# The last layer of a four-layer graph kernel: bursts of five units in place of three, placed by a table of bursts

## Chip, cores and metric

The kernel runs on one core of a Trainium2 chip. The metric is the device time of one launch in microseconds (us), as the median of the runs. Smaller is better.

## What is computed

The input is x, 16 batches of 1024 nodes with 64 features in float32, and one 1024 x 1024 adjacency matrix that all batches share. Four graph layers follow one another, each added to its input and layer-normalized. The change touches the fourth alone, layer 3. For each batch it computes (the reference, cut):

```python
def _gat_layer(h, mask, b):
    scores = jnp.einsum('...nd,...md->...nm', h, h)
    scores = jnp.where(mask, scores, NEG)
    attn = jax.nn.softmax(scores, axis=-1)
    return jnp.einsum('...nm,...md->...nd', attn, h) + b
mask = graph + jnp.eye(N, dtype=graph.dtype) > 0
h = jnp.einsum('bnc,hdc->bhnd', x, Wh)                  # 4 heads of 64
out_h = _gat_layer(h, mask[None, None], bh[None, :, None, :])
cat = jnp.transpose(out_h, (0, 2, 1, 3)).reshape(B, N, H * D)
z = jax.nn.leaky_relu(cat, negative_slope=0.2)
h2 = jnp.einsum('bnk,dk->bnd', z, Wo)
out2 = _gat_layer(h2, mask[None], bo)                   # the outer attention
z2 = jax.nn.leaky_relu(out2, negative_slope=0.2)
# layernorm of z2 with gamma and beta; then x = layernorm(x + that)
```

## The kernel before

The function that matters is `fast_path`. Layers 0 to 2 take the first 684 us. Layer 3 works on units. A unit is a tile of 128 x 1024 attention weights. It passes through three engines, and in the code each pass has its own step:

- `scores` (L1281 for heads, L1378 for the outer attention): TensorE (PE) makes the scores of the unit as two products with 64 rows each, which lie in the two halves of its array and run side by side. They go to a two-bank PSUM tile `s`, of which there are three. ScalarE (ACT) then takes the exponential into a tile `e` (L1285, L1383), with a shift that was worked out beforehand.
- the mask: VectorE (DVE) multiplies `e` with the adjacency `aT` (L1286; L1385 for outer units, there into a second tile `me`). For outer units a second DVE instruction, `add_up` (L1396), adds up the unmasked tile against the adjacency `aN` to get the softmax's denominators.
- `product` (L1293, L1405): PE multiplies the masked tile with the values, as two products with 64 columns each, and adds them up over 8 units in a PSUM tile `y`.

A batch has 32 head units (2 pairs of heads, 2 halves of the queries, 8 tiles of keys) and 8 outer units. The outer units of a batch stand among the head units of the next batch, since they need all of its heads. `tile e` has 9 buffers in a ring, used for `e`, for `me`, and in batch 0 for the adjacency tiles that `nodes_adj` loads again.

Between the units stand small tasks. `prep_x`, `prep_h` and `prep_sq` make the head features of a pair of batches; `shift_of` makes the shift (PE L1218, DVE L1222, a maximum over partitions on GpSimd L1224, and one small DVE instruction L1229); `project` (L1310 to L1320, then `leaky`) divides and leaves z; `z_T`, `h_2T`, `h_2v` (L1339, L1351, L1364) prepare the outer attention; `gather`, `layer`, `mean`, `centre`, `scale`, `affine`, `residual`, `finish` end a batch on DVE. `scale` asks ACT for a logarithm and an exponential (L702, L703). Most of them that use PE take one of the three `s` tiles.

The order on every engine of PE, ACT, DVE and GpSimd is the order in which the code issues, written out by hand. `run` takes units in bursts of three:

```python
catch_up()
made = [(unit[1], unit[0]()) for _, _, unit in burst if unit]   # scores, exp, mask
for b, p, _ in burst:
    tasks(mids, b, p)
drain()                          # the products of the burst before
```

So PE does three scores, then tasks listed as `mids`, then the three products of the burst before, then tasks listed as `slots`. `catch_up` runs, ahead of the next scores, what was left in the list `soon`: the last step of a shift, and the root and Newton step of a `scale`. The positions of tasks are counted in units, 40 to a batch. The outer unit comes after every second head unit from position 18 on (in the last batch after every one).

Of the kernel before, what the change touches and what calls it, by code (L numbers as in the profile page):

```python
# [8 lines left out]
F32 = mybir.dt.float32  # L9
F32R = mybir.dt.float32r  # L10
BF16 = mybir.dt.bfloat16
# [5 lines left out]
P = 128  # L17
# [561 lines left out]
def fast_path(  # L579
# [87 lines left out]

    soon = []
    in_order = {getattr(mybir.EngineType, e) for e in ("PE", "Activation", "DVE", "Pool")}
# [43 lines left out]
    def normalizing(y, sq, late):  # L713
# [15 lines left out]
        def scale():  # L729
            vs = small.tile([P, n], F32, tag="ln_vs", name="ln_vs")  # L730
            nc.vector.tensor_reduce(vs, sq, AX.X, ALU.add)
            ve = small.tile([P, n], F32, tag="ln_ve", name="ln_ve")
            nc.vector.tensor_scalar(ve, vs, 1.0 / D, LN_EPS, ALU.mult, ALU.add)
            rstd = small.tile([P, n], F32, tag="ln_rstd", name="ln_rstd")
            if late:
                nc.gpsimd.tensor_tensor(rstd, ve, neg_half, ALU.pow)
                return rstd
            root, step = inverse_root(rstd, ve)

            def first():  # L740
                root()
                soon.append(step)

            soon.append(first)
            return rstd
# [452 lines left out]
    def nodes_adj(c):  # L1198
        a_sb = l3.tile([P, N], I32, tag="e", name=f"adj3_{c}", bufs=9)
        nc.sync.dma_start(a_sb, adj_v[c])  # L1200
# [12 lines left out]
    def shift_of(key, sq):  # L1213
# [14 lines left out]
        def below():  # L1228
            nc.vector.tensor_scalar(sh, gtop, -1.0, HEADROOM, ALU.mult, ALU.add)  # L1229

# [41 lines left out]
    def heads(b, n):  # L1272
        held = {}

        def scores(k, h):
# [3 lines left out]
            for i in range(2):  # L1279
# [3 lines left out]
                )  # L1283
            e = l3.tile([P, 2, HALF], F32, tag="e", name="e", bufs=9)
            nc.scalar.activation(e, s, AF.Exp, bias=shifts[b, n])  # L1285
            nc.vector.tensor_tensor(e, e, bc_mid(aT[:, k, cols], 2), ALU.mult)  # L1286
            return e

        def product(k, h, e):
# [7 lines left out]
            if k == C - 1:  # L1297
                if h == 0:
                    held["y"] = l3.tile([P, N], F32, tag="y", name=f"yT_{b}_{n}")
                nc.scalar.copy(held["y"][:, h * HALF : (h + 1) * HALF], held[h])  # L1300

        def project(q):
# [5 lines left out]
            for j in range(CH):  # L1308
                c = q * CH + j
                nc.tensor.matmul(  # L1310
                    o[:, j // 2, j % 2, :], held["y"][:, c * P : (c + 1) * P], wb[:, n, :], start=True, stop=True,
                )
# [5 lines left out]
            for i in range(2):  # L1318
# [6 lines left out]

        units = [(lambda k=k, h=h: scores(k, h), lambda e, k=k, h=h: product(k, h, e), None)
                 for h in range(2) for k in range(C)]
        return units, project


    def prep_out(b):
# [28 lines left out]
        def h_2v():  # L1360
            v = l3.tile([P, C, D], F32, tag="h2v", name=f"h2v_{b}", bufs=1)
            pt = one_bank("ph2v").rearrange("p (c d) -> p c d", c=C)
            for c in range(C):
                nc.tensor.transpose(pt[:, c, :], hTs[b][0][:D, c // CH, c % CH * P : (c % CH + 1) * P], ident[:D, :D])  # L1364
            nc.vector.tensor_copy(v, pt)  # L1365
            vals["out", b] = v
# [3 lines left out]
    def head_out(b):  # L1370
        held = {}

        def scores(k):
            s = ps_s.tile([P, 2, HALF], F32, tag="s", name="s")
            hT = hTs[b][0]
            for i in range(2):
# [4 lines left out]
                )  # L1381
            e = l3.tile([P, 2, HALF], F32, tag="e", name="e", bufs=9)
            nc.scalar.activation(e, s, AF.Exp, bias=shifts[b])  # L1383
            m = l3.tile([P, 2, HALF], F32, tag="e", name="me", bufs=9)
            nc.vector.tensor_tensor(  # L1385
                m, e, aT[:, k, :].rearrange("p (i q) -> p i q", i=2), ALU.mult
            )
            return e, m

        def unit(k):  # L1390
            held[k], m = scores(k)
            return m

        def add_up(k):
            junk = l3.tile([P, N], BF16, tag="junk", name="junk", bufs=1)
            nc.vector.scalar_tensor_tensor(  # L1396
                junk, held.pop(k).rearrange("p i q -> p (i q)"), 1.0, aN[:, k, :], ALU.mult, ALU.mult,
                accum_out=sums[:, b, H, k : k + 1],
            )

# [55 lines left out]
        def finish():  # L1456
# [4 lines left out]
        units = [  # L1461
            (lambda k=k: unit(k), lambda e, k=k: product(k, e), lambda k=k: add_up(k)) for k in range(C)
        ]
# [150 lines left out]


    slots, mids = {}, {}
    work = [[heads(b, n) for n in range(NP)] for b in range(B)]
    outs = [(prep_out(b), head_out(b)) for b in range(B)]
    BURST = 3
    LAST = 40  # L1620
    E = B - 1

    def at(b, p, task, where=slots):
        where.setdefault((b, p), []).append(task)

    for c in range(C):
        convert = {}
        at(0, 2 * c, lambda c=c, convert=convert: convert.update(go=nodes_adj(c)))
        at(0, 2 * c + 5, lambda convert=convert: convert["go"]())
    for b in range(B):  # L1630
# [6 lines left out]
        ends = outs[b][1][1]  # L1637
        if b < E:
            places = [13, 22, 26, 33, LAST + 4, LAST + 7, LAST + 10, LAST + 13, LAST + 14]

            end = (41, 46, 49, 55) if b < E - 2 else (29, 31, 33, 39)
            places += [2 * LAST + p for p in (6, 8, 10, 11, 14, 23, 25, *end)]
        else:
            places = [13, 22, 26, 35, *[LAST - 1] * 5, *[LAST + 8] * 11]
        if b == E - 1:
            places[9:] = [LAST + 38, *[LAST + 39] * 4, *[2 * LAST + p for p in (3, 3, 3, 3, 3, 8)]]
        for task, p in zip(chain + ends, places):
            t = min(p // LAST, max(E - b, 0))
            at(b + t, p - t * LAST, task)


    ended = slots[E, LAST - 1]
    slots[E, LAST - 1] = [ended[i] for i in (5, 0, 1, 6, 2, 3, 7, 8, 9, 4)]
    ahead = []
    for b in range(0, B, 2):
        for t, p, task, where in (
            (-1, 16, lambda b=b: prep_x(b), slots),
            (-1, 20, lambda b=b: prep_h(b, 0, 0), mids), (-1, 23, lambda b=b: prep_sq(b, 0, 0), slots),
            (-1, 26, lambda b=b: prep_h(b, 0, 1), mids), (-1, 29, lambda b=b: prep_sq(b, 0, 1), slots),
            (-1, 25, lambda b=b: prep_v(b), slots),  # L1660
            (-1, 32, lambda b=b: shift_of((b, 0), hTs[b, 0][1]), slots),
            (-1, 36, lambda b=b: shift_of((b + 1, 0), hTs[b + 1, 0][1]), slots),
            (0, 2, lambda b=b: prep_h(b, 1, 0), mids), (0, 3, lambda b=b: prep_sq(b, 1, 0), slots),
            (0, 5, lambda b=b: prep_h(b, 1, 1), mids), (0, 8, lambda b=b: prep_sq(b, 1, 1), slots),
            (0, 11, lambda b=b: shift_of((b, 1), hTs[b, 1][1]), slots),
            (0, 20, lambda b=b: shift_of((b + 1, 1), hTs[b + 1, 1][1]), slots),
            (0, 19, lambda b=b: prep_v(b + 1), slots),
        ):
            if b + t < 0:
                ahead.append(task)  # L1670
            else:
                at(b + t, p, task, where)

    with tc.tile_pool(name="ps_g", bufs=1, space=bass.MemoryType.PSUM, reuse_waits="tile") as ps_g, tc.tile_pool(
# [13 lines left out]
        ending = gat_layer(later["w2"], "l2", True, extra, first, 5, True)  # L1688
    for p, task in zip((1, 4, 7, 10, 14, 16), ending):
        at(0, p, task)  # L1690

# [16 lines left out]

    queue = []
    for b in range(B):  # L1710
        units = work[b][0][0] + work[b][1][0]
        outer = outs[b - 1][1][0] if b else [None] * C
        for i, unit in enumerate(outer):
            units.insert(18 + (3 if b < E else 2) * i, unit)
        queue += [(b, p, unit) for p, unit in enumerate(units)]
    last = [(E, LAST + p, unit) for p, unit in enumerate(outs[E][1][0])]

    def run(queue):
        while queue:
            burst = []  # L1720
            while queue and sum(unit is not None for _, _, unit in burst) < BURST:
                burst.append(queue.pop(0))
            catch_up()
            made = [(unit[1], unit[0]()) for _, _, unit in burst if unit]
            for b, p, _ in burst:
                tasks(mids, b, p)
            drain()
            waiting.extend(lambda product=product, e=e: product(e) for product, e in made)
            if not queue:
                drain()  # L1730
            for b, p, _ in burst:
                tasks(slots, b, p)
            for _, _, unit in burst:
                if unit and unit[2]:
                    unit[2]()

    with tc.manual_schedule(engines=in_order):
        run(queue)
        run(last)
        for task in [catch_up, *slots[E, LAST + 8]]:  # L1740
            task()
            while soon:
                catch_up()

# [72 lines left out]
```

## Time and profile before

| | us |
|---|---|
| median of 3 runs | 2126.72 (2126.08 to 2129.75) |
| the profiled execution, its own time | 2126.6 |
| its span | 2124.7 |
| PE busy in the span | 1998.2 (94%) |
| DVE busy | 1858.1 (87%) |
| ACT busy | 1228.0 (58%) |
| stretch 684 to 1974, batches 0 to 14 of layer 3: PE busy of 1290 | 1267.7 |
| same stretch, DVE busy / ACT busy | 1113.9 / 791.9 |
| stretch 1974 to 2066, last batch: PE / DVE busy of 92 | 89.3 / 84.6 |
| stretch 2066 to the end: PE / DVE busy of 58.7 | 23.2 / 46.8 |

A row of the page such as "L1285 ACT ACTIVATE e<-s,shift ... x512 | 542.8, 1111 | 242.8 <-PE s L1281 237.4" reads: line 1285 of the kernel, on ACT, writes e from s and shift, 512 times; 542.8 us busy, 1111 ns each; ACT was idle for 242.8 us before these, mostly until PE had finished an s. PE is matmuls, PEld is TensorE's weight loads, which overlap them. PEld idle "<-issue" is time in which nothing that the profile shows was waited for. DMA hardly matters in layer 3 (1 to 12 GB/s).

### The profile page before, as it was taken

What the parts mean: (1) busy time and instruction counts of PE and PEld (TensorE: products, weight loads), DVE (VectorE), ACT (ScalarE), POOL (GpSimd) and SP (SyncE); (2) the same over time, 40 slices, a digit from 0 to 9 for tenths busy, and PEclk for the clock granted to TensorE, in tenths of its full rate; (3) what the DMA queues carried; (4) which work ended last, traced back from release to release, by engine and by line L of the source; (5) the groups of instructions that cost most, each with busy time, mean ns of one, the idle gap of its engine ahead of it and who ended that gap; (6) DMA issues with size and microseconds to landing.
All of it is one profiled execution on the core that took longest, in us unless ns stands there. A gap on an engine that the chain in (4) does not pass through costs nothing.

```text
span 2124.7 us, 26159 instructions
## 1 busy us (share of the span) xinstructions
PE 1998.2 (94%) x10065; PEld 845.2 (40%) x10065; DVE 1858.1 (87%) x3224; ACT 1228.0 (58%) x1965; POOL 55.6 (3%) x77
## 2 busy tenths in 40 slices
PE   7999979988898999999999999999999999999993
PEld 3444447753332333333333333333333333333331
DVE  5888989989999867898888898889889889889997
ACT  4355566555556756556656655655665666565541
POOL 0000000000000000000000000000000000000001
PEclk7999989999989999999999999999999999999997
DMA  6000000000000100000000000000000000000000
GB/s 165 1 1 1 1 1 1 1 0 1 1 1 31 50 1 1 1 1 6 6 1 6 1 6 6 1 6 1 6 6 1 6 1 6 6 1 6 6 6 12
DMA packets 23654, 18.89 MB, mean 9 GB/s; under 512 B 19361, under 2 KB 19426, under 8 KB 23522
## 3 DMA queue, kind: packets, MB, share of 16 engines
q1 hardware_dynamic: 23218, 17.11, 2.7%
q8 instruction: 81, 1.33, 0.3%
q14 instruction: 51, 0.42, 0.1%
q10 hardware_dynamic: 304, 0.03, 0.0%
HBM read 12.95 MB, written 4.19 MB: 8 GB/s over the span
## 4 chain that ended last, share of the span: by engine, by line
PE 68%; DVE 26%; ACT 4%; issue 1%; DMA 0%; POOL 0%; SPq 0%; POOLq 0%; DVEq 0%; ACTq 0%
PE y L1293 19%; PE s L1281 17%; DVE e L964 7%; PE y_l L976 6%; PE s L1378 5%; PE y L1405 4%; DVE e L1286 4%; PE po L1310 3%; PE u_l L988 3%; PE po L1567 3%; ACT e L1285 1%; DVE r L1576 1%; PE pzT L1339 1%; PE phT L1255 1%; DVE junk L1396 1%
## 5 line engine op out<-in xcount | busy, mean ns | idle before, releaser
L1285 ACT ACTIVATE e<-s,shift 128x1024 f32<-128x1024 f32 x512 | 542.8, 1111 | 242.8 <-PE s L1281 237.4
L1286 DVE TENSOR_TENSOR e<-e,aT 128x1024 f32<-128x1024 f32 x512 | 602.5, 1220 | 87.2 <-ACT e L1285 85.1
L1281 PE MATMUL s<-hT 64*128 64x512 f32 x2048 | 508.9, 610 | 16.0 <-DVE top L1222 8.8
L1293 PE MATMUL y<-e,vals 128*64 128x512 f32 x2048 | 490.6, 601 | 3.2 <-ACT yT L1300 1.3
L964 DVE SCALAR_TENSOR_TENSOR e<-G_l,q,aT 128x1024 f32<-128x1024 f32 x256 | 315.4, 1278 | 7.2 <-ACT G_l L945 7.2
L976 PE MATMUL y_l<-e,vals_l 128*64 128x512 f32 x1024 | 263.6, 639 | 23.8 <-DVE e L964 23.0
L1281 PEld LDWEIGHTS s<-hT 64*128 64x128 f32 x2048 | 181.8, 186 | 256.3 <-issue 169.2
L1293 PEld LDWEIGHTS y<-e,vals 128*64 128x64 f32 x2048 | 131.0, 136 | 330.6 <-issue 257.7
L1383 ACT ACTIVATE e<-s,shift 128x1024 f32<-128x1024 f32 x128 | 141.7, 1112 | 84.8 <-PE s L1378 74.9
L1385 DVE TENSOR_TENSOR me<-e,aT 128x1024 f32<-128x1024 f32 x128 | 155.8, 1220 | 16.8 <-ACT e L1383 16.5
L1396 DVE SCALAR_TENSOR_TENSOR junk<-e,aN 128x1024 bf16<-128x1024 f32 x128 | 156.0, 1219 | 0.2
L1405 PE MATMUL y<-me,h2v 128*64 128x512 f32 x512 | 135.3, 609 | 10.6 <-DVE me L1385 10.4
L1378 PE MATMUL s<-h2T 64*128 64x512 f32 x512 | 136.3, 610 | 4.6 <-DVE h2v L1365 4.4
L976 PEld LDWEIGHTS y_l<-e,vals_l 128*64 128x64 f32 x1024 | 65.6, 142 | 162.2 <-issue 75.0
L1567 PE MATMUL po<-hi,aR 128*128 128x512 f32 x256 | 101.9, 398 | 2.7 <-ACT hi L1552 1.1
L1567 PE MATMUL po<-lo,aR 128*128 128x512 f32 x256 | 99.8, 390 | 0.0
L775 ACT ACTIVATE x<-m,bn_shift,bn_rstd 128x64 f32<-128x64 f32 x256 | 88.2, 429 | 0.0
L1340 ACT COPY zT<-pzT 128x1024 f32<-128x1024 f32 x32 | 32.4, 1013 | 78.4 <-PE pzT L1339 78.4
L1310 PEld LDWEIGHTS po<-wb,yT 128*128 128x128 f32 x512 | 62.0, 190 | 34.0 <-issue 21.1
L1310 PE MATMUL po<-wb,yT 128*128 128x130 f32 x512 | 73.8, 287 | 1.3 <-ACT e L1285 1.2
L1378 PEld LDWEIGHTS s<-h2T 64*128 64x128 f32 x512 | 46.6, 186 | 63.7 <-issue 41.4
L1405 PEld LDWEIGHTS y<-me,h2v 128*64 128x64 f32 x512 | 32.7, 137 | 93.8 <-issue 56.1
(214 smaller groups left out, 2003.7 us busy)
## 6 DMA issues: line engine op xcount, KB each, us to landing
adj<-in_adj_dram SPq DMA_DIRECT2D x16, 512.0 KB, 4.5
x<-in_x_dram SPq DMA_DIRECT2D x16, 256.0 KB, 5.0
out_dram<-res SPq DMA_DIRECT2D x16, 256.0 KB, 2.0
wl<-in_L_gnn_Wh_dram SPq DMA_DIRECT2D x2, 64.0 KB, 4.8
wo<-in_L_gnn_Wo_dram SPq DMA_DIRECT2D x1, 64.0 KB, 4.4
l_wd<-in_L_gnn_W_dram ACTq DMA_DIRECT2D x2, 16.0 KB, 4.7
l_wd<-in_L_gnn_W_dram SPq DMA_DIRECT2D x2, 16.0 KB, 2.1
bo<-in_L_gnn_bo_dram SPq DMA_DIRECT2D x1, 32.0 KB, 3.1
```

The source lines that it names most:

```text
L964: nc.vector.scalar_tensor_tensor(e, G[b - b % 2][:, b % 2, :], pq[b - b % 2][1][:, k, b % 2 : b % 2 + 1], aT[:, k, :], ALU.max, ALU.mult,)
L976: nc.tensor.matmul(held["y"][h * D : (h + 1) * D, :], vals[b][:, k, :], e[:, h * HALF : (h + 1) * HALF], start=(k == 0), stop=(k == C - 1),)
L1281: nc.tensor.matmul(s[:, i, :], hT[rows, k * P : (k + 1) * P], hT[rows, cols], start=True, stop=True)
L1285: nc.scalar.activation(e, s, AF.Exp, bias=shifts[b, n])
L1286: nc.vector.tensor_tensor(e, e, bc_mid(aT[:, k, cols], 2), ALU.mult)
L1293: nc.tensor.matmul(held[h][i * D : (i + 1) * D, :], vals[b][:, k, :], e[:, i, :], start=(k == 0), stop=(k == C - 1),)
L1310: nc.tensor.matmul(o[:, j // 2, j % 2, :], held["y"][:, c * P : (c + 1) * P], wb[:, n, :], start=True, stop=True,)
L1378: nc.tensor.matmul(s[:, i, :], hT[rows, (i + k // CH) % 2, k % CH * P : (k % CH + 1) * P], hT[rows, 0, :], start=True, stop=True,)
L1385: nc.vector.tensor_tensor(m, e, aT[:, k, :].rearrange("p (i q) -> p i q", i=2), ALU.mult)
L1396: nc.vector.scalar_tensor_tensor(junk, held.pop(k).rearrange("p i q -> p (i q)"), 1.0, aN[:, k, :], ALU.mult, ALU.mult, accum_out=sums[:, ...
L1405: nc.tensor.matmul(held["o"][h * D : (h + 1) * D, :], vals["out", b][:, k, :], e[:, h, :], start=(k == 0), stop=(k == C - 1),)
L1567: nc.tensor.matmul(po.rearrange("p q k f -> p (q k f)"), aR[:, k, ic * P : (ic + 1) * P], e[:, k].rearrange("p q k f -> p (q k f)"), start ...
```

## The change

Layer 3 is staged anew. Its core (lines with "..." are left out):

```diff
-            nc.vector.tensor_scalar(sh, gtop, -1.0, HEADROOM, ALU.mult, ALU.add)
+            nc.scalar.activation(sh, gtop, AF.Identity, bias=headroom, scale=-1.0)
...
-            e = l3.tile([P, 2, HALF], F32, tag="e", name="e", bufs=9)
+            e = l3.tile([P, 2, HALF], F32, tag="e", name="e", bufs=11)
             nc.scalar.activation(e, s, AF.Exp, bias=shifts[b, n])
-            nc.vector.tensor_tensor(e, e, bc_mid(aT[:, k, cols], 2), ALU.mult)
+            return e
+
+        def mask(k, h, e):
+            nc.vector.tensor_tensor(e, e, bc_mid(aT[:, k, h * HALF : (h + 1) * HALF], 2), ALU.mult)
             return e
...
-                if h == 0:
-                    held["y"] = l3.tile([P, N], F32, tag="y", name=f"yT_{b}_{n}")
-                nc.scalar.copy(held["y"][:, h * HALF : (h + 1) * HALF], held[h])
+                held["y"] = l3.tile([P, HALF], F32, tag="y", name=f"yT_{b}_{n}_{h}", bufs=1)
+                nc.scalar.copy(held["y"], held[h])
...
-            nc.vector.tensor_copy(v, pt)
+            nc.scalar.copy(v, pt)
             vals["out", b] = v
...
+        def mask(k, e):
+            m = e
+            if b < B - 1:
+                add_up(k, e)
+            else:
+                m = l3.tile([P, 2, HALF], F32, tag="e", name="me", bufs=11)
+            nc.vector.tensor_tensor(m, e, aT[:, k, :].rearrange("p (i q) -> p i q", i=2), ALU.mult)
+            if b == B - 1:
+                add_up(k, e)
             return m
...
+    for b in range(B):
+        units = work[b][0][0] + work[b][1][0]
+        outer = outs[b - 1][1][0] if b else []
+        for j in range(BURSTS):
+            n = 5 if j < 4 else 3
+            burst, units = units[:n], units[n:]
+            if j >= 4:
+                for i, unit in enumerate(outer[2 * (j - 4) : 2 * (j - 3)]):
+                    burst.insert(1 + 2 * i, unit)
+            plan.append((b, j, burst))
+    units = outs[E][1][0]
+    last = [(E, BURSTS, units[:5]), (E, BURSTS + 1, units[5:])]
+
+    def run(plan):
+        for b, j, burst in plan:
             catch_up()
+            made = [(unit, unit[0]()) for unit in burst]
+            tasks(mids, b, j)
+            while roots:
+                roots.pop(0)()
             drain()
+            made = [(product, mask(e)) for (_, mask, product), e in made]
             waiting.extend(lambda product=product, e=e: product(e) for product, e in made)
-            if not queue:
+            if (b, j, burst) == plan[-1]:
                 drain()
+            tasks(slots, b, j)
```

A batch is now 8 bursts, numbered 0 to 7. The first four hold 5 head units each, the last four 3 head units and 2 outer ones. The positions of the small tasks are burst numbers, in `mids` or `slots`. Most tasks that use PE (`prep_x`, `prep_h`, `shift_of`, `project`, the first `z_T`, `h_2T`, `h_2v`, `gather`) are in `mids`, between the scores and the products. The masks of a burst are issued to DVE after the small tasks in `mids`. The root of a `scale` goes to a list `roots`, which runs after the `mids`. Outer tiles are masked in place, apart from the last batch, and the tile that `add_up` writes its product to, which nobody reads, shares the buffer of `project`. Each half of a head pair is copied out of PSUM to a tile of its own, with one buffer, and projected from there. The shift's last step and the copy of `h_2v` go from DVE to ACT. The number of `s` tiles stays three.

## The prediction

> **What bounds the kernel now.** I read the stretches first, then the waits of PE, then the timeline of a few bursts, then the groups.
>
> ```profile
> 684.00:1974.00 1290.00, 1267.71 (x6175) 489.30 (x6175) 1113.91 (x1660) 791.93 (x944) 26.98 (x44) 1.00 0.02 5
> 1974.00:2066.00 92.00, 89.26 (x420) 33.31 (x417) 84.58 (x130) 50.68 (x58) 0.35 (x1) 1.00 0.01 3
> 2066.00:2124.70 58.70, 23.15 (x102) 8.40 (x100) 46.82 (x80) 11.07 (x12) 7.86 (x5) 0.75 0.04 15
> ```
>
> Columns: stretch, length, busy PE, PEld, DVE, ACT, POOL, granted clock. From 684 to 1974 us PE is busy 98% at clock 1.00, DVE 86%, ACT 61%: PE sets the pace. From 1974 on DVE is at 92% and takes over; after 2066 it is a DVE chain. A busy PE is not a PE at its peak, so the timeline of two bursts without small tasks:
>
> ```profile
> 695.02 2.85 PE L1281 MATMUL s<-hT 64*128 64x512 f32 x12
> 697.80 2.79 PE L1293 MATMUL y<-e,vals 128*64 128x512 f32 x12
> 700.53 2.85 PE L1281 MATMUL s<-hT 64*128 64x512 f32 x12
> 701.06 0.19 PEld L1281 LDWEIGHTS s<-hT 64*128 64x128 f32 x2 [0.24 <-issue]
> 701.49 0.19 PEld L1281 LDWEIGHTS s<-hT 64*128 64x128 f32 x2 [0.24 <-issue]
> 703.30 0.20 PEld L1293 LDWEIGHTS y<-e,vals 128*64 128x64 f32 x4 [0.76 <-DVE aN L1203]
> ```
>
> Within a phase the weight loads follow at 0.43 us (701.06 to 701.49), two to a unit: a unit costs 0.855 us in scores and 0.855 in products. But a phase of three scores starts 2.77 to 2.78 us ahead of the products (700.53 to 703.30), and three products take 2.73 (697.80 to 700.53), where 3 x 0.855 = 2.565. So the two switches of a burst cost 0.21 + 0.17 = 0.38 us, in which the loads show 0.76 to 0.81 idle instead of 0.24. PE has no other wait that counts:
>
> ```profile
> PE s L1281 <- DVE top L1222: 8.8, 8, 1.9
> PE s L1378 <- DVE h2v L1365: 4.4, 4, 1.1
> PE s L1281 <- DVE h2v L1365: 4.4, 4, 1.1
> ```
>
> That is 17.6 us in the stretch 690 to 2000: small tasks whose PSUM tile DVE gave back late. Comparing each PE phase with the shortest of its kind, I count about 30 us over it in layer 3, of which 5 in the last batch.
>
> **The change: the switches.** Before, layer 3 has 16 x 32 + 15 x 8 = 632 units in bursts of three and the last 8 in three bursts: some 213 phases of scores. The order of the changed program has 129 of scores and 128 of products. 84 bursts fewer x 0.38 = **-32 us**. The number of small tasks on PE stays; they still split one switch each (the same 1.08 us for `project`, 0.28 for a shift), as cheap between scores and products as before the scores.
>
> Here a rule bears: the Trainium skill, "TensorEngine Tiling (Array Packing)", Key Properties, says that changing the tiling mode, not just the tile, drains TensorE. Scores are 64-row tiles and products 64-column tiles, so each phase change is one. It gives no figure; "TensorE: Matmul & The Clock Gate" (Single matmul latency, Back-to-back issue gap) has (398 + N)/2.4 ns alone against N/2.4 + 2.5 in a row, that is 163 ns for a drain. By the page 84 x 2 x 0.163 = 27 us, by the trace 32. I take the trace.
>
> **PSUM tiles.** A burst of five needs five `s` tiles of three. The fourth waits for the first exponential, the fifth for the second. From the trace:
>
> ```profile
> 1012.97 2.85 PE L1281 MATMUL s<-hT 64*128 64x512 f32 x12
> 1014.14 3.12 ACT L1285 ACTIVATE e<-s,shift 128x1024 f32<-128x1024 f32 x3 [2.38 <-PE s L1281]
> 1015.31 0.19 PEld L1255 LDWEIGHTS phT<-xT,whT 64*128 64x128 f32 x2 [0.33 <-ACT e L1285]
> 1015.64 1.02 PE L1255 MATMUL phT<-xT,whT 64*128 64x512 f32 x4
> ```
>
> The first exponential starts 1.17 us after the scores and takes 1.11; the next follow at 1.005 (3.12 - 1.11 over 2). They end 2.28, 3.29, 4.29, 5.30, 6.30 after the burst's start; a load follows 0.06 later. A fourth user of the ring (here phT) started at 2.67, just where three scores and an entry end: no loss. The fifth would start at 3.53 and may load at 3.35: no loss. The first task in `mids` may load at 4.35 and comes at about 4.5: none. A second one may load at 5.36: after a `project` (1.08) or `z_T` (1.02) it is later anyway, but after a short one it waits: pn then po 0.5 us, `h_2v` (0.43) then phT or pn 0.35, `gather` then `h_2T` 0.2. That is 1.05 us a batch x 15 = 16 us. Add 0.3 a batch for the accumulator of a half that ACT must copy out (rows of that kind before: 0.29 to 0.40), 5 us.
>
> A rule speaks against the change here: the Trainium skill, "Perfetto Trace Analysis", Optimization Strategy: a gap that repeats on the engine that should be saturated can mean too little PSUM for the next tile. Before, the 26 waits of phT loads for an exponential sum to 9.0 us, 0.35 each, and PE itself shows none. By the rule, 0.35 in each of 129 bursts would be 45 us, and the sum would be +13. By the row it hides under the running matmuls; I take 16 and keep 45 as the far end.
>
> **Waits that go.** The root of `scale` ran ahead of the scores' exponentials and ACT waited for DVE there (L702 on L733: 55.3 us in 13 times, up to 5.5); now it stands behind five exponentials. Masks no longer stand ahead of the tasks that free PSUM, so the 17.6 us of rows above should go. With the phases of the stalled kind this is most of the 25 us that I counted outside the last batch. So stalls: -25 + 16 + 5 = -4.
>
> **DVE.** Full stretch: 465.6 of 530 us in six batches (945 to 1475), 77.6 a batch. L1229 (0.15 x 3) and `h_2v` (0.68) leave: 76.5. Per burst: a mask costs 1.167 (3.50 for three), an outer unit with sum 2.45. Bursts 0 to 3: 5.8 plus small work of 3.6, 2.8, 3.1, 4.2; bursts 4 to 7: 8.4 plus 1.7, 2.3, 1.4, 1.8. So 9.4, 8.6, 8.9, 10.0, 10.1, 10.7, 9.8, 10.2 (1.2 over the batch's 76.5 in all, as small rows overlap). PE's bursts are 5 x 1.71 + 0.38 = 8.93 plus small tasks: about 10.6, 11.1, 11.7, 11.0, 10.4, 10.4, 9.1, 10.2. In the last four DVE has 40.8 to PE's 40.1. DVE must wait for `mids` of PE (about 5.6 into the burst) before it may mask, and the masks are wanted 4.4 into the next burst at the first unit, 7.8 at the fifth. From 5.6 that leaves 12 to 13 us for 10.2 of work (`project` 1.8 + masks 8.4): slack of some 2 to 3 us, enough for a lag of 0.7. So DVE does not show in an ordinary batch. Queued behind the masks are the `slots` tasks and, with the next `mids`, what frees their PSUM tiles; these are due 1.7 us into the following burst and come about 2 us ahead of it.
>
> **ACT.** It gets three instructions of 128x1 a batch (nearest row: ACT L702, 0.21; bounds 0.15 to 0.25) and a 128x512 copy (0.59, L1300): 1.2 us a batch. ACT works some 53 of 87 us a batch, and five exponentials end 6.3 us into a burst of about 10; the shift's step needs GpSimd's maximum, which follows DVE's by 0.35 to 1.2 and comes before the next burst except in burst 7, where it is level. Cost 0; if the cover goes, 0.5 us x 15 = 8. In place of two buffers, one tile in place: no DVE time. The two more buffers of `e` hold two bursts and one: an exponential needs the buffer of a product two bursts back, long done. Queues of SP and POOL keep their instructions: 8 loads of the adjacency, one per burst, still wait for a free `e` (landing 4.5 us, conversion 1.3 one burst later).
>
> **Start and end.** At 684 no products exist: the first two bursts are ten exponentials and two `prep_h` instead of six, so the first product comes at about 699 instead of 692.3; PE gains 3.4 us of scores in it: **+3**. In the last batch the adds and the ends of two batches meet: adding the DVE work burst by burst as above, with 43.6 us in bursts 4 to 7, DVE has the last mask ready 91 us after the batch's start and PE ends at 92; before 2064.6 - 1974.2 = 90.4. So of the 2 us that the switches save there nothing remains and 2 to 3 are lost: **+4** against the count above. The chain after it (8 masks and 8 sums, then the closing on DVE) is the same work: 0, bounds -2 to +2.
>
> **Sum.** -32 - 4 + 3 + 4 = -29 from the profiled execution's 2126.6, which is 0.1 under the median of the runs. 2126.6 - 29 = 2097.6, rounded **2098**.
>
> **Rivals.**
> 1. *The PSUM ring decides.* If ACT starts its first exponential late in a burst (a z copy or a yT copy in front), all five scores move by that. From 0.25 us per burst (32 / 129) it eats the gain; at the rule's 0.35 in each burst, on top of the 20 of small tasks: -32 - 25 + 45 + 21 + 7 = +16, about 2143. For: ACT rows of yT wait for PE at the burst's end. Against: a yT copy (0.59) ends before 1.17. Chance 0.09.
> 2. *DVE decides.* In-order waits for `mids` cost DVE about 1 us in each of 8 bursts; 76.5 + 8 = 84.5 a batch, level with PE's 85. With 1.5 more it holds a batch at 86.5: gain 1 us x 15, less the 7 of both ends: about 2115 to 2122. For: outer bursts are level. Against: the slack worked out above. Chance 0.15.
> 3. *No stall comes.* The tasks behind short ones find their tile: -32 - 25 + 7 = -50, 2077. Chance 0.16.
> 4. *The switch is no switch* (the 0.38 goes with something else): within 4 us of before. Chance 0.05.
>
> **Numbers.** Likeliest (2084 to 2110) 0.55, rival 3 0.16, rival 2 0.15, no change 0.05, slower 0.09. The range takes the likeliest, most of 3 and half of 2: 2076 to 2117. A difference of 0.2% (4.3 us) is about what a measurement can tell: faster 0.87, same 0.04, slower 0.09.
>
> **What would show it.** Right: about 129 phases of scores, five units of a burst in 4.3 to 4.4 us and 8.9 to 9.0 from burst to burst without tasks; a batch in about 85.4 us (87.6 before, between 748.2 and 1974.2); the PE rows that wait for DVE top and h2v gone; new waits of po, phT, ph2T loads for e L1286. Wrong: PE waiting for e of the mask (rival 2), or s waiting for e of the exponential in most bursts (rival 1).

## The result, and the profile after

The changed kernel takes 2103.18 us (median of 4 runs, 2102.57 to 2106.58), the kernel before beside it 2126.78 (2126.08 to 2129.75). The ratio is 0.9886, with a 95% interval of 0.9872 to 0.99: faster by 23.6 us. The profiled execution took 2103.7 us, its span is 2101.4. Layer 3 starts 1.6 us later in this profile (685.8 instead of 684.2), although next to nothing ahead of it was changed (the shift steps of the first heads, which run in layer 2, went to ACT). From its start to the end of the span layer 3 takes 1415.7 us instead of 1440.6, which is 24.9 us less. The rest of this text counts from the start of layer 3.

The stretches after, with the same columns as before (length, busy PE, PEld, DVE, ACT, POOL, granted clock):

```profile
685.80:1949.10 1263.30, 1241.87 (x6163) 501.43 (x6162) 1099.03 (x1598) 800.35 (x1001) 40.18 (x44) 1.00 0.02 6
1949.10:2042.50 93.40, 88.12 (x427) 35.14 (x426) 86.92 (x127) 50.81 (x60) 0.35 (x1) 1.00 0.01 4
2042.50:2101.40 58.90, 24.64 (x107) 8.84 (x105) 46.75 (x83) 11.85 (x14) 7.87 (x5) 0.74 0.04 15
```

PE is again busy 98% in the long stretch, and its number of instructions hardly differs (6163 and 6175), but its busy time fell by 25.8 us. Nearly all that was won lay inside "busy": the profile counts the time of a switch between the two tile shapes as busy. The last batch (93.4 instead of 92.0) and the chain after it (58.9 instead of 58.7) gained nothing.

The scores of a burst without outer units, two small tasks, and the products of the burst before it, in PE's timeline:

```profile
1359.45 4.56 PE L1282 MATMUL s<-hT 64*128 64x512 f32 x20
1363.94 1.16 PE L1312 MATMUL po<-wb,yT 128*128 128x130 f32 x8
1365.03 1.13 PE L1256 MATMUL phT<-xT,whT 64*128 64x512 f32 x4
1366.09 4.51 PE L1297 MATMUL y<-e,vals 128*64 128x512 f32 x20
1370.54 1.09 PE L1343 MATMUL pzT<-ident,z 128*128 128x128 f32 x8
```

Five scores take 4.49 us up to the next task (1359.45 to 1363.94) and five products 4.45 (1366.09 to 1370.54): 8.94 for ten passes, of which 10 x 0.855 = 8.55 are the passes and the rest, 0.39, the two switches.

That the change of tile shape is what costs, the traces show where a small task has the shape of the phase ahead of it. `phT` has the shape of the scores (64*128). Three scores take 2.68 us to a `phT` that follows them in each of 28 places before (750 to 1970 us), and 2.77 or more to everything else; and a `phT` right behind scores takes 0.96, while behind `project` (po, 128*128) it takes 1.06, as above. Before:

```profile
1012.97 2.85 PE L1281 MATMUL s<-hT 64*128 64x512 f32 x12
1015.64 1.02 PE L1255 MATMUL phT<-xT,whT 64*128 64x512 f32 x4
1016.60 1.08 PE L1293 MATMUL y<-e,vals 128*64 128x512 f32 x4
```

In the same way three products take 2.63 instead of 2.73 where `ph2T` follows, which has their shape (128*64).

The waits of PE from 684 to 2000 us (time, times, longest):

```profile
PE po L1312 <- ACT e L1286: 9.4, 16, 0.6
PE y L1297 <- ACT yT L1303: 3.8, 8, 1.0
PE ph2T L1355 <- ACT e L1286: 2.8, 13, 0.2
PE pn L1219 <- ACT e L1387: 2.1, 7, 0.3
PE phT L1256 <- ACT e L1387: 2.1, 7, 0.3
```

The rows for DVE's top and h2v (17.6 us before) are gone. In their place small tasks wait for an exponential: `project` behind the norms, `h_2T` behind `gather`, and whatever stands behind `h_2v`. The first and the last of these places read so in PE's timeline:

```profile
1383.51 4.56 PE L1282 MATMUL s<-hT 64*128 64x512 f32 x20
1388.01 0.25 PE L1219 MATMUL pn<-pair_ones,h2sq 128*128 128x2 bf16 x4
1388.87 1.16 PE L1312 MATMUL po<-wb,yT 128*128 128x130 f32 x8 [0.61 <-ACT e L1286]
...
1398.80 0.67 PE L1368 MATMUL ph2v<-ident,h2T 64*128 64x64 f32 x8
1399.76 0.34 PE L1219 MATMUL pn<-pair_ones,hsq 128*128 128x2 bf16 x8 [0.30 <-ACT e L1387]
```

`pn` comes 4.50 us after the burst's start and `po` at 5.36, when the fourth exponential has freed its PSUM tile. Behind `h_2v` the same (burst from 1394.40, `pn` at 1399.76: 5.36).

Adding up PE's phases, per batch over batches 2 to 13:

| us a batch | before | after | difference |
|---|---|---|---|
| scores and products | 75.19 | 71.85 | -3.34 |
| small tasks of PE, with their waits | 12.34 | 13.98 | +1.64 |
| a batch | 87.53 | 85.83 | -1.70 |

Over the whole layer the differences are: batch 0 +0.2, batch 1 -5.1, batches 2 to 14 -21.8, last batch and chain +1.8, in sum -24.9.

### The profile page after: what moved, and what is told of

Same layout as the page of the kernel before. It is cut to its first block, busy times and chain, and to the rows that moved or that the text cites. A ratio compares the mean times of both kernels' runs of the same rounds, so it can differ in the third digit from the quotient of the medians.

```text
span 2101.4 us, 26433 instructions
## 1 busy us (share of the span) xinstructions
PE 1969.2 (94%) x10065; PEld 858.0 (41%) x10065; DVE 1845.0 (88%) x3160; ACT 1237.7 (59%) x2029; POOL 69.7 (3%) x77
## 4 chain that ended last, share of the span: by engine, by line
PE 45%; DVE 41%; ACT 10%; issue 3%; DMA 0%; POOL 0%; SPq 0%; POOLq 0%; DVEq 0%; ACTq 0%
DVE e L1290 12%; PE y L1297 11%; PE s L1282 8%; DVE e L965 7%; ACT e L1286 6%; PE y_l L977 6%; DVE junk L1392 4%; DVE e L1403 4%; PE u_l L989 3%; PE po L1574 3%; PE po L1312 2%; PE y L1412 2%; ACT e L1387 2%; DVE v L1322 1%; PE s L1382 1%
## 5 line engine op out<-in xcount | busy, mean ns | idle before, releaser
L1290 DVE TENSOR_TENSOR e<-e,aT 128x1024 f32<-128x1024 f32 x512 | 600.4, 1217 | 1.7 <-ACT e L1286 1.6
L1282 PE MATMUL s<-hT 64*128 64x512 f32 x2048 | 495.1, 603 | 1.2 <-ACT e L1286 0.9
L1282 PEld LDWEIGHTS s<-hT 64*128 64x128 f32 x2048 | 185.7, 186 | 278.0 <-issue 138.9
L1403 DVE TENSOR_TENSOR e<-e,aT 128x1024 f32<-128x1024 f32 x120 | 147.0, 1225 | 6.4
L1382 PE MATMUL s<-h2T 64*128 64x512 f32 x512 | 131.6, 595 | 0.0
L1412 PE MATMUL y<-e,h2v 128*64 128x512 f32 x480 | 123.4, 592 | 2.7 <-DVE e L1403 2.7
L1225 POOL PARTITION_ALL_REDUCE gtop<-top x48 | 42.5, 885 | 1367.0 <-DVE top L1223 1298.8
L1316 DVE COPY sums<-po 128x8 f32<-128x8 f32 x64 | 10.9, 170 | 71.8 <-PE po L1312 71.8
```

The lines of the kernel that those rows point to most:

```text
L1282: nc.tensor.matmul(s[:, i, :], hT[rows, k * P : (k + 1) * P], hT[rows, cols], start=True, stop=True)
L1290: nc.vector.tensor_tensor(e, e, bc_mid(aT[:, k, h * HALF : (h + 1) * HALF], 2), ALU.mult)
L1382: nc.tensor.matmul(s[:, i, :], hT[rows, (i + k // CH) % 2, k % CH * P : (k % CH + 1) * P], hT[rows, 0, :], start=True, stop=True,)
L1403: nc.vector.tensor_tensor(m, e, aT[:, k, :].rearrange("p (i q) -> p i q", i=2), ALU.mult)
```

## The experiments

All are edits of the changed kernel and are timed against the kernel before, whose median was 2128.34, 2127.71 and 2128.91 us in the three sessions. A difference to the change is taken from its 2103.18 us, so 1 to 2 us of it can be the session. "Layer 3" is from the first instruction of the layer to the end of the span, in the profile.

**Is it the number of bursts? (e1_split)** Each burst of five is cut into three and two, the tasks with the second part; all else is as changed.

```diff
+            if len(burst) == 5:
+                plan.append((b, None, burst[:3]))
+                burst = burst[3:]
```

> The changed kernel with every burst of five run as a burst of three and a burst of two; the small tasks stay with the second part. 124 more phases of scores and of products. Theory (each burst's two switches of TensorE cost 0.38 us): +47 us from switches; the small tasks then follow two scores instead of five, so their waits for a PSUM tile (about 1.5 us a batch) go: -20 to -23. Together about +26 on the changed kernel's 2103: 2125 to 2133. Scores and products without stalls should take 13.33 x 0.38-like costs again: about 3.0 us a batch more. Rival (the 0.38 belongs to something else than the switch, the gain came from waits): the PSUM waits go and nothing is added: about 2082.

Measured: 2136.45 us, ratio 1.0036 (1.0027 to 1.0046). Layer 3 takes 1448.4, +32.8 against the change. One cut burst in PE's timeline:

```profile
1351.94 1.13 PE L1282 MATMUL s<-hT 64*128 64x512 f32 x4
...
1354.72 1.08 PE L1412 MATMUL y<-e,h2v 128*64 128x512 f32 x4
...
1356.59 1.13 PE L1382 MATMUL s<-h2T 64*128 64x512 f32 x4
...
1358.51 0.35 PE L1219 MATMUL pn<-pair_ones,hsq 128*128 128x2 bf16 x8
1358.79 1.08 PE L1297 MATMUL y<-e,vals 128*64 128x512 f32 x4
...
1361.52 1.13 PE L1282 MATMUL s<-hT 64*128 64x512 f32 x4
```

From 1351.94 to 1361.52 are 9.58 us, of which the norms at 1358.51 take 0.28: 9.30 for ten passes, where the uncut burst has 8.94. Over batches 2 to 13, scores and products take 74.99 a batch, +3.14 for 8 more bursts: 0.39 each. The small tasks fall by 1.12 to 12.86, since a task behind two scores finds its PSUM tile free more often (the waits of po fall from 9.4 to 2.8 us, those of ph2T, pn and phT are gone). So fewer switches are what was won, and waits for the ring are what was paid for them. The sum over the layer is above 16 x (3.14 - 1.12) = 32.3 by only 0.5. The cut bursts also show where the old stalls went: from batch 2 to the last no phase of scores in this trace is longer than 2.78 us for three or 1.92 for two, while before they reached 4.49 for three. So the length of the bursts did not end these stalls; something else in the change did, the new places of the tasks, masks and roots above all (e3_roots and e5_masks bear on two of them).

**Can the ring's waits be ordered away? (e2_order)** The three tiles stay. `h_2T` goes ahead of `gather`; `project` and `prep_x` go ahead of the outer shift, `prep_h` ahead of `h_2v`; and one head shift moves from burst 4 to burst 6. A long task then stands where a short one stood.

```diff
+    for key, todo in mids.items():
+        if key[1] == 2:
+            todo.reverse()
...
-            (0, 4, lambda b=b: shift_of((b + 1, 1), hTs[b + 1, 1][1]), mids),
+            (0, 6, lambda b=b: shift_of((b + 1, 1), hTs[b + 1, 1][1]), mids),
...
+    for key, todo in mids.items():
+        if key[1] in (3, 4):
+            todo.append(todo.pop(0))
```

> The changed kernel with the order of tasks in mids changed so that no short one stands ahead of another: h_2T ahead of gather, project (and prep_x) ahead of the outer shift, prep_h ahead of h_2v, and the second pair's shift of even batches moved from burst 4 to burst 6, where it stands alone. Theory (the second task of a burst gets its PSUM tile 5.35 us after the burst's start, when the fourth exponential is done, and waits if the first was short): 0.65 + 0.38 + 0.52 us a batch go, 15 batches: -20 to -23 us, 2080 to 2083. Rival (the wait moves: VectorE gets its small tasks later, or products wait for masks): 2100 to 2104.

Measured: 2079.99 us, ratio 0.9766 (0.9743 to 0.9788); layer 3 1391.9, -23.8 against the change. The waits of PE from 684 to 2000 in this kernel:

```profile
PE y L1297 <- ACT yT L1303: 1.1, 2, 0.7
PE s L1282 <- ACT e L1286: 0.9, 1, 0.9
PE s L1282 <- DVE v L1039: 0.3, 1, 0.3
PE po L1312 <- ACT e L1286: 0.2, 1, 0.2
```

The same work on the same tiles, and the waits of po, ph2T, pn and phT are gone but for 0.2 us. Per batch the small tasks cost 12.52 instead of 13.98, 1.46 less: 21.9 us over 15 batches. Most of the other 1.9 lies in the products of burst 5, described under e9_acc. A burst with the norms moved, from its scores to its products:

```profile
1359.25 4.56 PE L1282 MATMUL s<-hT 64*128 64x512 f32 x20
1363.75 1.94 PE L1355 MATMUL ph2T<-zT,woT 128*64 128x512 f32 x8
1365.61 0.66 PE L1425 MATMUL po<-ident,y2T 128*128 128x128 f32 x4
1366.11 0.34 PE L1219 MATMUL pn<-pair_ones,hsq 128*128 128x2 bf16 x8
1366.38 4.51 PE L1297 MATMUL y<-e,vals 128*64 128x512 f32 x20
```

The norms (`pn`) now follow 6.86 us after the burst's start, behind tasks long enough for their tile to be free: no row in it waits.

**Roots ahead again (e3_roots).** The root of a `scale` goes back to the list that runs ahead of the next exponentials.

```diff
-            roots.append(first)
+            soon.append(first)
...
+            while soon:
+                catch_up()
```

> The changed kernel with the root of the normalizations back ahead of the next burst's exponentials. In the changed kernel's trace VectorE delivers the variance 2.0 to 3.1 us into burst 2 and 3.5 to 5.5 us into burst 5, the first exponential starts at 1.2. Theory (a root ahead holds up the exponentials, and the fourth and fifth scores then wait for PSUM): up to 1.5 + 3.5 us in each of 13 batches, less what VectorE gains on TensorE meanwhile: +20 to +65, about 2140. Rival (exponentials have room): 2102 to 2106.

Measured: 2217.86 us, ratio 1.0416 (1.0389 to 1.0442), +115. ACT's row from 760 to 2040:

```profile
ACT ln_rstd L703 <- DVE ln_ve L734: 103.6, 25, 8.0
```

The direction was right, the size not. Of ACT's 103.6 us PE hides a part, as I had expected: it waits 57.2 for exponentials in the same stretch, in this row and one of 14.9 for `s` of L1282:

```profile
PE s L1382 <- ACT e L1286: 42.3, 13, 4.2
```

The other part is the clock. PE's granted clock lies at half for 81.9 us of this stretch; before and after the change it is 1.00 from 700 to 2000 us throughout. If PE does half its work in such time, that is 41 us more (an estimate): 57 + 41 = 98 of the 101 us by which batches 2 to 14 grew; the last batch and its chain took 15 more. Burst 5's scores last up to 10.77 us instead of 4.49. ACT waits longer than before the change (55.3): in the changed kernel DVE has the variance (L734) only 2.0 to 5.5 us into the burst.

**ACT's two new steps back on DVE (e4_dve).** The last step of the shift and the copy of `h_2v`.

```diff
-            nc.scalar.activation(sh, gtop, AF.Identity, bias=headroom, scale=-1.0)
+            nc.vector.tensor_scalar(sh, gtop, -1.0, HEADROOM, ALU.mult, ALU.add)
...
-            nc.scalar.copy(v, pt)
+            nc.vector.tensor_copy(v, pt)
```

> The changed kernel with the shift's last step and the copy of h_2v back on VectorE. The sum of the prediction gave this edit 1.1 us a batch of VectorE's time, hidden, and the move a value of 0: 2102 to 2105. Other theory: it is the order that counts. The step of the outer shift then stands behind VectorE's work for burst 3, which ends 4.6 to 5.5 us into burst 4, while the second exponential of burst 4 needs it at 2.2: the scores of burst 4 lose 2 to 3 us in each of 15 batches: +30 to +45, about 2140.

Measured: 2190.97 us, ratio 1.0287 (1.0261 to 1.0313): +88, twice what the higher expectation had (for the reason see e7_shift). The waits from 760 to 2000 name the shift:

```profile
ACT e L1387 <- DVE shift L1230: 35.8, 14, 3.7
PE s L1282 <- ACT e L1387: 32.3, 13, 3.4
```

**The shift's step alone (e7_shift).** Only the first of the two edits of e4_dve.

> The changed kernel with only the shift's last step back on VectorE; the copy of h_2v stays on ScalarE. With both back the time was 2191. Theory (the step of the outer shift stands behind VectorE's work of burst 3 and holds up the second exponential of burst 4; the row there is 35.8 us in 14 times): +35 to +45 us of the +88, 2140 to 2148; the rest belongs to h_2v, for which VectorE waits ahead of the masks of burst 4 (50.4 us in 14). Rival (h_2v alone matters): 2103 to 2110. Rival (the shift alone matters): 2185 or more.

Measured: 2187.77 us, ratio 1.029 (1.0268 to 1.0312): +84.6, so one instruction of 128x1 makes nearly all of e4_dve's loss. Its timeline, all engines, lines left out:

```profile
1332.81 0.35 POOL L1225 PARTITION_ALL_REDUCE gtop<-top  x1 [72.69 <-DVE top L1223]
...
1342.67 0.69 DVE L727 TENSOR_TENSOR v<-v,ln_mean 128x512 f32<-128x512 f32 x1
1343.40 0.69 DVE L728 TENSOR_TENSOR m<-v 128x512 f32<-128x512 f32 x1
1344.01 0.14 DVE L1230 TENSOR_SCALAR shift<-gtop 128x1 f32<-128x1 f32 x1
...
1344.25 1.11 ACT L1387 ACTIVATE e<-s,shift 128x1024 f32<-128x1024 f32 x1 [2.51 <-DVE shift L1230]
1345.41 1.86 PE L1282 MATMUL s<-hT 64*128 64x512 f32 x4 [2.27 <-ACT e L1387]
```

GpSimd has the maximum at 1333.16. DVE takes its 0.14 us step at 1344.01, 10.85 us later, since masks (5.76 us for five) and steps of `project` and of the normalization stand ahead of it. The exponential waits 2.51 us, PE 2.27 behind that. In batches 2 to 14 burst 4's scores last 6.8 to 8.7 us instead of 4.4, and in every other batch burst 3 is late as well.

Waits make only half of the 85 us. From 760 to 2000 PE waits 41.8 us for exponentials; right behind such bursts its granted clock falls to half for 3.4 or 6.8 us at a time (the last line is a stretch, with the columns of the stretches above; its clock is 0.50):

```profile
PE s L1282 <- ACT e L1387: 29.9, 13, 3.1
PE s L1282 <- ACT e L1286: 11.9, 7, 1.7
...
1072.60:1079.40 6.80, 6.80 (x32) 2.73 (x31) 5.04 (x7) 3.24 (x5) 1.17 (x1) 0.50 0.00 0
```

The products that started at 1074.22 took 7.02 us instead of 4.44. In all 84.3 us between 700 and 2000 ran at half clock. At half the work that costs 42 us (an estimate), and 41.8 + 42 is the loss within 2 us. In e4_dve it is 44.1 us of waits and 68.4 us at half clock. In the other nine kernels of this text the clock is 1.00 throughout that stretch. PE's longest wait there is 1.9 us (the kernel before), against 3.1 to 4.2 in e3_roots, e4_dve and e7_shift. That the waits bring the clock down is likely from this, but no run tests it. The expectation of 35 to 45 us fits the waits; the fall of the clock it did not have.

**Masks ahead of the small tasks (e5_masks).** The line that makes the masks moves up, ahead of `mids`.

```diff
+            made = [(product, mask(e)) for (_, mask, product), e in made]
             tasks(mids, b, j)
...
-            made = [(product, mask(e)) for (_, mask, product), e in made]
```

> The changed kernel with the masks of a burst issued to VectorE ahead of the small tasks in mids, as before the change. Theory of the prediction (masks ahead keep the small tasks' PSUM tiles, and TensorE waits for them as in the 17.6 us of waits before): +10 to +20 us, about 2118, with rows of TensorE waiting for VectorE's sums, v or top. Rival (a burst of five leaves VectorE time for both, and without the wait for mids it even runs ahead): 2098 to 2106.

Measured: 2136.24 us, ratio 1.0039 (1.0025 to 1.0052): +33. Of the rows I had looked for, one came back, with 11.5 us, and rows of other engines were far larger (760 to 2000):

```profile
DVE e L1290 <- ACT e L1286: 152.4, 91, 5.2
ACT shift L1230 <- POOL gtop L1225: 127.1, 35, 6.9
PE s L1282 <- DVE v L1322: 11.5, 15, 0.8
```

DVE now waits for exponentials before it may find a shift's maximum; the maximum comes late to GpSimd, and ACT stands at the head of the next burst on a step of 0.30 us, with five exponentials behind it. After the change this ACT row is 19.4 us.

**Both of these undone (e10_both).** The edits of e5_masks and e7_shift together.

> The changed kernel with both orders of VectorE undone: masks ahead of the small tasks in mids, and the shift's last step on VectorE. Alone they cost 33 and 85 us. Theory (both delay the same thing, the shift that ScalarE needs: with masks ahead, the maximum is found late, and its last step stands in the same queue): the costs do not add, since the step follows the maximum at once when masks stand ahead; the time lies near the dearer of the two or below, 2136 to 2190. Rival (two separate losses): 2220.

Measured: 2120.54 us, ratio 0.995 (0.9933 to 0.9968), only 17 us above the change, less than either alone (+33, +85). ACT's large rows for the shift, of GpSimd in e5_masks and of DVE in e7_shift, are both gone. The clock stays at 1.00. Of what remains, 11.9 us show as short waits of PE for tiles that DVE frees behind masks:

```profile
PE s L1282 <- DVE v L1322: 11.9, 14, 1.0
```

**How much room has DVE? (e6_load)** Every second `add_up` is issued twice and takes the same sum again: 4 more instructions a batch, 4.9 us.

```diff
+                if k % 2 == 0:
+                    add_up(k, e)
```

> The changed kernel with every second sum of an outer unit done twice on VectorE (the same number is written twice), in all batches but the last: one 128x1024 instruction (1.22 us) more in each of bursts 4 to 7, 4.9 us a batch, which brings VectorE from 76.5 to about 81.4 of 85.8 us. Theory (VectorE has 2 to 4 us of slack in a burst and waits for TensorE 1.7 us at each project): at most 1 us a batch, 2103 to 2118. Rival (VectorE sets the pace in the outer bursts): 4.9 x 15 = +74 us, 2177.

Measured: 2125.79 us, ratio 0.999 (0.9982 to 0.9999), +22.6, where DVE as the bound would have given 15 x 4.9 = 74. So PE sets the pace, and 4.9 us are somewhat more than DVE has to spare. From batch 4 on odd batches take 88.6 and even ones 85.7, where the change has 86.0 and 85.7, and the last batch with its chain takes 8.6 more. In the odd batches PE waits for masks of outer tiles:

```profile
PE y L1414 <- DVE e L1405: 10.6, 13, 1.3
```

**The start (e8_start).** e2_order, and the first burst of layer 3 cut into three and two.

```diff
+            if b == j == 0:
+                plan.append((b, None, burst[:3]))
+                burst = burst[3:]
```

> The kernel with the reordered tasks (2080) and the very first burst of layer 3 run as three and two, tasks with the second part. Theory (the prediction's +3 us at the start: with two bursts of five ahead of the first product TensorE has nothing to do for about 3 us): 2077 to 2079. Rival (the start is bound elsewhere): 2080 to 2081.

Measured: 2078.6 us, ratio 0.9767 (0.9753 to 0.978). The first product comes 6.2 us after the layer's start (13.2 after the change, 8.1 before), and batch 0 takes 62.6 instead of 64.0. Layer 3 as a whole is 1390.9 against e2_order's 1391.9. A difference of 1 us is below what the runs resolve.

**The accumulator (e9_acc).** e8_start, and in burst 5 the two outer units stand side by side, so that a product of the next half comes later.

```diff
-                    burst.insert(1 + 2 * i, unit)
+                    burst.insert(1 + (i if j == 5 else 2 * i), unit)
```

> The kernel with reordered tasks and the shorter first burst (2078.6), and in burst 5 of every batch the two outer units stand side by side, behind the first head unit, instead of one behind each of the first two. Theory (the last unit of one half and the first of the next share a PSUM accumulator, and one product of 0.855 us between them is too short for ScalarE's copy: 0.35 or 0.63 us over the ordinary 4.44 in the products of that burst in every batch): two products between them hide it, -0.5 x 15 = -7 us, 2071 to 2073. Rival (the wait is not the copy, or ScalarE is late anyway): 2077 to 2080.

Measured: 2075.7 us, ratio 0.9754 (0.9733 to 0.9775), the lowest median of all, but its interval and those of e2_order and e8_start overlap. The wait itself, in the change, in the products of burst 5:

```profile
1418.99 1.08 PE L1297 MATMUL y<-e,vals 128*64 128x512 f32 x4
1419.90 1.03 PE L1412 MATMUL y<-e,h2v 128*64 128x512 f32 x4
1421.34 1.08 PE L1297 MATMUL y<-e,vals 128*64 128x512 f32 x4 [0.41 <-ACT yT L1303]
...
1424.06 1.13 PE L1282 MATMUL s<-hT 64*128 64x512 f32 x4
```

The phase takes 5.07 us here (1418.99 to 1424.06) and 4.79 in the batches between, instead of 4.44. In e8_start, on which this edit stands, it is 4.79 in every batch: the order of e2_order had already taken 0.28 from every other one. With the edit it takes 4.44 in every batch. That is 0.35 a batch, 5.0 us from batch 1 to 14, and not the 7 of the expectation. The layer gained 3.1 of them, since the last batch and its chain took 1.9 more.

## Why the prediction was right, step by step

The prediction said 2098 with a range of 2076 to 2117, and faster. 2103.2 lies in the range, 5 us above the likeliest value; the likeliest case (the switches win, the ring takes a part back) is the one that came. That it is as near as 5 us is in part luck: the ring and the accumulator cost about 8 us more than their terms, the stalls and the two ends about 4 less.

- **Switches, -32.** Right. Two neighbouring switches cost 0.38 in the trace before and 0.39 in e1_split, which put more of them back than the change had taken away. 5.33 bursts fewer a batch x 0.383 = 2.04 of the 3.34 us that scores and products lost.
- **Stalls that go, -25.** Right as a sum. Scores and products lost 3.34 a batch; take off 2.04 for switches and put back about 0.5 for the accumulator, and 1.8 a batch are left, some 27 us over 15 batches. The trace before has the same: over batches 2 to 13 its phases of three scores and three products lie 1.8 us a batch above 2.78 and 2.73. The rows for top and h2v did go. e1_split shows that the longer bursts are not what ended them, and e3_roots and e5_masks that the old places of the roots and masks do not fit the new bursts. Which single move ended which stall was not run.
- **PSUM ring, +16: the term that was mis-sized.** The places were right, and so was the time at which the tile for a second small task comes free (5.36 after the burst's start). The waits were set down too short. From a first task at 4.5 to a second one at 5.36 there are 0.86 us, however short the first is; the prediction's task times and waits (0.43 + 0.35 for `h_2v`, for one) leave only 0.7 to 0.8. In the change `pn`, `h_2v` and `gather` take 0.86, 0.96 and 0.87 with what they make the next one wait; in e2_order, without waits, 0.17, 0.62 and 0.54. The small tasks cost 1.64 a batch more than before, and e2_order takes 1.46 of it away by order alone: 22 us of waits where the prediction had 16.
- **Accumulator, 0.3 a batch.** Right in kind, low in size: 0.35 in one batch and 0.63 in the next, 7 us instead of 5.
- **Start +3 and last batch +4.** In sum near. Batch 0 and the last batch with the chain came out at +0.2 and +1.8, although both have fewer switches (9 bursts less, 3.4 us). So the ends themselves cost about 5 us where the prediction had 7. e8_start moved batch 0 by 1.4 us, half of the 3.
- **DVE.** Right: it does not show in an ordinary batch. (The 77.6 us a batch are slightly high: 530 us are 6.06 batches and not six, which makes it 76.9.) In e6_load, of 4.9 us more a batch only 1.2 came through over batches 2 to 13 (87.07 instead of 85.83). Even in e2_order, where PE's batch is 84.25, PE waits for DVE once from 684 to 2000, for 0.3 us.
- **ACT's new steps, 0.** As a cost nothing in the change speaks against it, though the step takes ACT about 0.3 us and not 0.15 to 0.25. As a reading of the edit it failed: the prediction's "Cost 0" treats the move of the shift's step as one of 0.15 to 0.25 us, with or without cover worth 8 us. Its place in the queue was worth 85 us in this order (e7_shift), half of it in waits and half in the clock. The prediction asked what ACT gains in work, and not what the step would have waited for on DVE once the masks stand behind the small tasks.
- **Row or rule.** At both places the row held. The trace's 0.38 for two switches came back as 0.39; the 163 ns a drain, an estimate that the prediction worked out from the Trainium skill's page "TensorE: Matmul & The Clock Gate" (Single matmul latency, Back-to-back issue gap), would have been 0.33. The gap for want of PSUM did not come in each of 129 bursts (45 us), only where a short task stands in front (22 us). The prediction's +13 for that rule sets the 45 against the 32 alone; with its other terms it is the +16 of its first rival.

Of the rivals, the ring deciding (2143) was half a mechanism: it took 22 us and not 45 + 21, and PE's scores waited for an exponential once, for 0.9 us. "No stall comes" (2077) describes e2_order, at 2080. That the switch is no switch is ruled out by e1_split and by the phases next to a task of their own shape, and DVE as the bound by e6_load. Left untested are the two more buffers of `e`, the masks in place and the halves of `y`, which came with the change; the prediction gave them nothing, and no wait named above points to them.

## What to carry to other kernels

Longer bursts of one tile shape on PE saved a fixed cost for each switch here, and two phases of the trace were enough to count it. What they cost was decided by order, in the queues and in the ring: with three PSUM tiles a short task in front made the next one wait, and a longer one in front made the wait vanish without a further tile. A tiny step is priced by what stands ahead of it in its engine's queue at that place and by what waits for it, not by its duration; so weigh two moves that share a queue together, since either alone may lose what both together win. And when PE has begun to wait, look at the granted clock before you put the whole loss down to the wait.

## What was not expected of the hardware

- Undoing two moves cost 17 us, undoing one of them 33 and the other 85. They were a pair: late masks on DVE and the shift's step on ACT.
- In the three runs whose scores waited 3 to 4 us for an exponential, the granted clock of PE fell to half for 68 to 84 us between 700 and 2000 us, and about doubled the loss (e7_shift). What sets it off is not shown.
- ACT can stand 6.9 us at the head of a burst on an instruction of 0.30 us that waits for GpSimd (e5_masks).
- In a profile, the layer's start moves with little or no change ahead of it: by 1.6 us between before and after, and by 7.9 us between e2_order and e1_split, which are the same program up to there. Between before and after it arises in the first 80 us; between the other two 5 us do, and 3 come later, still ahead of layer 3. Spans of single profiles are compared better from the layer's own start.
